# Moving the loads of a scan's B and C rows from SP's queue to ScalarE's

## The chip, the cores and the metric

The kernel runs on one core of a Trainium2 chip. The metric is the device time of one execution in microseconds (us). The engines are called PE (matmul; PEld are its weight loads), DVE or VectorE, ACT or ScalarE, POOL or GpSimd, and SP, which computes nothing and issues transfers (DMAs). ScalarE issues some transfers too, from the same in-order queue that holds its activations.

## What is computed

A stack of eight gated blocks on x (4 batches of 512 tokens by 512 features), with a context of 512 by 256 per batch. Each block adds tanh(gate) times a sub-layer of the normalised x:

```python
x = x + tanh(g_xattn[0]) * L0_xattn(ctx, ln(x))    # a selective scan (Mamba)
x = x + tanh(g_ffn[0])   * L0_ffn(ln(x))           # gated MLP, 2:4 sparsified
x = x + tanh(g_xattn[1]) * L1_xattn(ln(x), ctx)    # attention of the context on itself
x = x + tanh(g_ffn[1])   * L1_ffn(ln(x))           # gated MLP, ternary weights
x = x + tanh(g_xattn[2]) * L2_xattn(ctx, ln(x))    # a selective scan again
x = x + tanh(g_ffn[2])   * L2_ffn(ln(x))           # gated MLP, fp8 weights
x = x + tanh(g_xattn[3]) * L3_xattn(ln(x), ctx)    # 16-head cross attention
x = x + tanh(g_ffn[3])   * L3_ffn(ln(x))           # quantised MLP
```

The part that matters here is the scan of blocks 0 and 4. For each batch, with 512 inner channels and 16 states:

```python
state = state * exp(d_t[..., None] * A) + (d_t * u_t)[..., None] * B_t[:, None, :]
y_t   = einsum('ben,bn->be', state, C_t)
```

d and u are per channel and time; B and C are per state and time, the same for all channels. The scan depends on the context alone, not on x; x enters through the factor silu(ln(x)) that its result is multiplied with.

## The kernel before

There are eight scans: two layers (0 and 1, for blocks 0 and 4) by four batches. A tile is 128 partitions by 512 times, so a scan has 4 channel tiles (d = 0 to 3) by 16 states (n = 0 to 15), 64 steps. One step is `state` and a sum: ScalarE writes exp(d * A) into a PSUM bank (line 570), POOL multiplies du with the row of B (line 571, into `db`), VectorE runs the recurrence along time (line 572, in place in PSUM) and multiplies with the row of C (line 573), and POOL adds the product to y (line 590). The bank comes from a pool of two (`mbps`), which the preparation of later scans (`mamba_pre`) shares.

The rows of B and C for state n are loaded by `bc_tile` (lines 561 to 565): one transfer that reads 2 rows of 512 from DRAM and writes them to all 128 partitions, 512 KB, into a tile with the tag `bc`. There are two such buffers (line 1217). A load for state n therefore waits until VectorE's last product (line 573, d = 3) of state n - 2 has been computed, and POOL's first product of state n waits for the load. The four steps of one state use one `bc` tile.

The first scan (layer 0, batch 0) runs in the prologue in another form, `mamba_scan_pe`, with PE adding up y. The other seven are `mamba_scan`, a generator. They are side work: the main path (attention and MLPs of the batch at hand) calls `tick` after each of its pieces, and `tick` takes steps from the side list at a given rate, 1.2 units a step. Side work gets a priority 1000 places behind the main path (`BEHIND`, from the second phase on). The framework then puts each engine's instructions in an order by a planning run of its own: of what is ready, the instruction with the lowest priority number goes first. What it planned is a fixed order per engine; on the chip each engine, SP and ScalarE's issues included, works its list off in that order and waits where something isn't there.

A scan has to be complete before the head that uses it starts (`Head.start` calls `finish`), which happens in the last matmuls of the MLP or the attention of the batch before. Six heads follow each other while scans run; from about 2390 us on there are none left, and the last heads and the quantised MLPs run alone.

SP issues nearly all transfers in one queue: weights (`unit`, `unit8`, `plain`, lines 259 to 305), stores and loads of the scans' preparation (`copy`, line 247), the scans' d, du and y (line 583), attention's keys and values (line 905), and `bc`. ScalarE issues 188 stores (`keep`, line 252), each right after the activation that wrote its data.

Of the kernel before, what the change touches and what calls it, by code (L numbers as in the profile page):

```python
# [24 lines left out]
NST = 16  # L25
# [50 lines left out]
def tile_flamingo(ctx: ExitStack, tc: tile.TileContext, I, out):  # L76
    nc = tc.nc
    v, s, g, pe, sy = nc.vector, nc.scalar, nc.gpsimd, nc.tensor, nc.sync
# [26 lines left out]
    def nm(base):  # L105
        uid[0] += 1
        return f"{base}_{uid[0]}"

    def T(p, shape, dt, tag, name=None):
        return p.tile(shape, dt, tag=tag, name=nm(name or tag))  # L110
# [95 lines left out]
    for l in range(2):  # L206
# [5 lines left out]
        c = cp.tile([128, 20], F32, name=f"cw{l}")  # L212
# [30 lines left out]
    def copy(dst, src):  # L243

        behind = COPIES if phase[0] else COPIES_FIRST
        tc.cur_priority += behind
        sy.dma_start(dst, src)
        tc.cur_priority -= behind
# [309 lines left out]
            yield 3.4  # L558
        mst[l, b] = bcd, sc

    def bc_tile(bcd, n, p, bufs):

        bc = p.tile([128, 2, 512], F32, tag="bc", name=nm("bc"), bufs=bufs)
        sy.dma_start(bc, bcd.rearrange("(c n) l -> n c l", c=2)[n].partition_broadcast(128))
        return bc

    def state(l, b, n, d, dt, du, bc, db):

        ps = mbps()
        s.activation(ps, dt, AF.Exp, scale=nA[l][:, d * 16 + n : d * 16 + n + 1])  # L570
        g.tensor_tensor(db, du, bc[:, 0], op=MUL)
        v.tensor_tensor_scan(ps, ps, db, 0.0, MUL, ADD)
        v.tensor_tensor(db, ps, bc[:, 1], op=MUL)  # L573

    def mamba_scan(l, b, mp, red):

        M = lambda tag: T(mp, [128, 512], F32, tag)
        bcd, sc = mst[l, b]
        dts, us, ys = [], [], []
        for d in range(4):  # L580
            for tag, r, src in (("dt", dts, sc[d][0]), ("du", us, sc[d][1]), ("y", ys, ysc[l, b][d])):
                x = M(tag)
                copy(x, src)
                r.append(x)
        for n in range(NST):
            bc = bc_tile(bcd, n, mp, mbufs["bc"])
            for d in range(4):
                db = T(mp, [128, 512], F32, "db", f"db{l}{b}x")
                state(l, b, n, d, dts[d], us[d], bc, db)
                red(d).tensor_tensor(ys[d], ys[d], db, op=ADD)  # L590
                yield 1.2
        for d in range(4):
            copy(ysc[l, b][d], ys[d])

    def mamba_scan_pe(l, b, pp):

        bcd, sc = mst[l, b]
        yp = [bank("y", "yp") for d in range(4)]
        for q in range(0, NST, 4):
            bcs = [bc_tile(bcd, n, pp, 6) for n in range(q, q + 4)]  # L600
            for d in range(4):
                if q == 0:
                    pe.matmul(yp[d], ident, sc[d][2], start=True, stop=False)
                for n in range(q, q + 4):
                    db = pp.tile([128, 512], F32, tag="db", name=nm(f"db{l}{b}x"), bufs=5)
                    state(l, b, n, d, sc[d][0], sc[d][1], bcs[n - q], db)
                    pe.matmul(yp[d], ident, db, start=False, stop=n == NST - 1)
                    yield
        ysc[l, b] = yp
# [606 lines left out]
    mp = mctx.enter_context(tc.tile_pool(name="m", bufs=4))  # L1216
    mbufs = {"bc": 2, "mt": 4, "db": 3, "fc": 2, "fw": 2, "kn": 4, "fv": 4, "sq": 1}
# [50 lines left out]
    for h in heads[1:]:  # L1268
        side.append(((h.l, h.b), mamba_scan(h.l, h.b, mp, on_g)))
        pres.append(((h.l, h.b, "pre"), mamba_pre(h.l, h.b, mp)))  # L1270
# [108 lines left out]
```

## Time and profile before

| | |
|---|---|
| time, median of 3 runs (lowest, highest) | 3700.73 us (3695.64, 3701.61) |
| the profiled execution | 3697.43 us, of it 3695.6 us from the first to the last instruction |
| granted TensorE clock, mean | 0.929 |
| busy in 190 to 2400 us (2210 us): PE, DVE, ACT, POOL | 1816.50, 1729.76, 1193.44, 1432.27 us |
| busy in 2400 to 3696 us (1296 us): PE, DVE, ACT, POOL | 1164.84, 639.38, 674.50, 225.29 us |
| exponential of line 570, mean | 690 ns |
| POOL's product with B, median | 1.27 to 1.29 us |
| VectorE's recurrence and product with C, median | 1.22 and 0.68 us |
| issue of a `bc` load on SP, shortest / median / longest | 359 / 371 / 1463 ns |
| a `bc` load, issue to landing, shortest / median / longest | 4.6 / 6.1 / 11.1 us |

How to read what the prediction shows: a row of the waits names the waiting engine, the tile it was about to write and its line, then what ended the wait; the numbers are us in total, how many times, and the longest. `SPq` and `ACTq` are transfers issued on SP's and ScalarE's queue. `db11x` is the product tile of the scan of layer 1, batch 1. A timeline row has the start, the length, the engine, the line, the operation, output <- inputs, and in brackets the engine's idle time before it with what ended it. Rows of stretches have their own legend where they stand.

### The profile page before, as it was taken

The numbers are of one execution on the slowest core, as the hardware profiler recorded it, in microseconds if no ns is written. First come the engines' busy times: TensorE is split into PE (matmuls) and PEld (weight loads), VectorE is DVE, ScalarE is ACT, GpSimd is POOL, SyncE is SP. The second block draws the span as 40 slices with busy tenths as digits, with TensorE's granted clock in tenths as the row PEclk, the third lists the DMA queues.
The fourth block names the chain that finished last, engine by engine and source line by source line (L and its number), as shares of the span: only waits on it lengthen the run. The fifth ranks groups of instructions, "written<-read, shape, count | busy, mean of one in ns | idle before, by whom it ended". The sixth has DMA issues, their size and how long they took to land. (4 is left out here: it accounts for less than half of the span.)

```text
span 3695.6 us, 40240 instructions
## 1 busy us (share of the span) xinstructions
PE 3121.5 (84%) x12216; PEld 1982.6 (54%) x12216; DVE 2535.7 (69%) x4162; ACT 1971.7 (53%) x4371; POOL 1762.6 (48%) x1387
## 2 busy tenths in 40 slices
PE   7787778787886798988878887799998898998995
PEld 3365355563654554574646544475766554664542
DVE  7968766987779868887587888754334446554437
ACT  6455365453632766645544756543435666456644
POOL 4616865757656656646475699600101122212112
PEclk8898899898998999999889999899999999999997
DMA  7667559776755664585656553386654343454311
GB/s 267 235 236 266 175 188 315 252 233 192 239 180 196 214 192 126 177 281 154 229 189 211 179 158 94 111 293 228 227 199 157 109 125 120 150 169 135 114 37 36
DMA packets 303737, 682.62 MB, mean 185 GB/s; under 512 B 31104, under 2 KB 32512, under 8 KB 303520
## 3 DMA queue, kind: packets, MB, share of 16 engines
q1 hardware_dynamic: 278240, 634.43, 52.8%
q10 hardware_dynamic: 25280, 45.63, 3.3%
q8 instruction: 97, 1.59, 0.2%
q14 instruction: 120, 0.98, 0.1%
HBM read 514.97 MB, written 164.95 MB: 184 GB/s over the span
## 5 line engine op out<-in xcount | busy, mean ns | idle before, releaser
L570 ACT ACTIVATE mb<-dt,nA 128x512 f32<-128x512 f32 x512 | 347.9, 690 | 419.6 <-DVE db03x L573 61.5
L323 POOL TENSOR_TENSOR sm<-sm,mhalf 128x8 f32<-128x8 f32 (+4 forms) x96 | 140.6, 1465 | 521.4 <-DVE sm L353 208.5
L663 PE MATMUL gate<-xT,w 128*128 128x512 f32 x624 | 267.0, 428 | 71.1 <-DVE t L730 30.3
L961 PE MATMUL po<-pt,v 128*128 128x512 f32 x512 | 269.6, 628 | 52.7 <-ACT pt L803 49.8
L786 PE MATMUL S<-k,q 128*128 128x512 f32 x512 | 269.2, 627 | 31.7 <-ACT P L793 23.2
L392 PE MATMUL acc<-w,hf 128*128 128x512 f32 x512 | 240.3, 628 | 44.5 <-DVE x L419 14.1
L664 PE MATMUL gate<-xT,w 128*128 128x512 f32 x624 | 257.3, 413 | 1.0 <-DVE xT L257 1.0
L793 ACT ACTIVATE P<-S,st,sm 128x512 f32<-128x512 f32 x256 | 200.3, 785 | 98.4 <-DVE st L791 94.6
L663 PE MATMUL up<-xT,w 128*128 128x512 f32 x624 | 247.5, 397 | 0.6 <-DVE h L731 0.4
L664 PE MATMUL up<-xT,w 128*128 128x512 f32 x624 | 247.1, 396 | 0.0
L787 DVE TENSOR_REDUCE st<-S 128x1 f32<-128x512 f32 x256 | 173.9, 685 | 95.6 <-PE S L786 94.4
L979 PE MATMUL down<-wo,h 128*128 128x512 f32 x512 | 234.4, 609 | 0.8 <-DVE h L970 0.5
L323 POOL TENSOR_TENSOR sml<-sml,mhalf 128x1 f32<-128x1 f32 x32 | 18.5, 579 | 425.1 <-DVE sml L1150 218.4
L392 PEld LDWEIGHTS acc<-w,hf 128*128 128x128 f32 x512 | 102.0, 202 | 177.5 <-issue 120.8
L801 PEld LDWEIGHTS pT<-ident,P 128*128 128x128 f32 x1024 | 127.6, 144 | 128.1 <-issue 64.1
L961 PEld LDWEIGHTS po<-pt,v 128*128 128x128 f32 x512 | 89.4, 194 | 185.1 <-ACT pt L803 146.1
L801 PE MATMUL pT<-ident,P 128*128 128x128 f32 x1024 | 158.4, 280 | 33.3 <-ACT P L793 27.2
L663 PEld LDWEIGHTS gate<-xT,w 128*128 128x128 f32 x624 | 125.0, 200 | 112.4 <-issue 32.4
L803 ACT COPY pt<-pT 128x512 f32<-128x512 f32 x256 | 143.8, 588 | 64.4 <-PE pT L801 63.9
L666 PE MATMUL gate<-xT,w 128*128 128x512 f32 x432 | 174.9, 405 | 3.8 <-POOL w L257 3.8
L666 PE MATMUL up<-xT,w 128*128 128x512 f32 x432 | 169.3, 392 | 0.0
L392 PE MATMUL acc<-w,h 128*128 128x512 f32 x352 | 161.9, 612 | 8.7 <-DVE x L426 5.1
(290 smaller groups left out, 9058.1 us busy)
## 6 DMA issues: line engine op xcount, KB each, us to landing
bc<-dbc SPq DMA_DIRECT2D x128, 512.0 KB, 6.1
w<-dL_g SPq DMA_DIRECT2D x81, 512.0 KB, 5.5
w<-dL_u SPq DMA_DIRECT2D x81, 512.0 KB, 5.1
w<-in_L_d_dram SPq DMA_DIRECT2D x60, 512.0 KB, 5.4
w<-dL_q SPq DMA_DIRECT2D x48, 512.0 KB, 5.3
w<-dL_gu SPq DMA_DIRECT2D x36, 512.0 KB, 4.9
rep<-in_L_b_dram SPq DMA_DIRECT2D x65, 256.0 KB, 3.8
dv<-fv ACTq DMA_DIRECT2D x64, 256.0 KB, 4.7
```

The source lines that it names most:

```text
L323: g.tensor_tensor(a, a, mhalf[:, :n], op=ALU.pow)
L392: pe.matmul(ps, h[:, c], w, start=first, stop=last)
L570: s.activation(ps, dt, AF.Exp, scale=nA[l][:, d * 16 + n : d * 16 + n + 1])
L663: pe.matmul(ps, wh[:, c], xT[k][:, 0], start=k == 0, stop=False)
L664: pe.matmul(ps, wh[:, c], xT[k][:, 1], start=False, stop=wl is None and k == 3)
L666: pe.matmul(ps, wl[:, c], xT[k][:, 0], start=False, stop=k == 3)
L786: pe.matmul(ps, q[:, c], k, start=True, stop=True)
L787: v.tensor_reduce(st[:, t : t + 1], ps, AX.X, ALU.max, negate=True)
L793: s.activation(p, ps, AF.Exp, scale=r, bias=m, accum_out=st[:, 8 + t : 9 + t])
L801: pe.transpose(ps[:, t * 128 : t * 128 + 128], pt[t][:, kt * 128 : kt * 128 + 128], ident)
L961: pe.matmul(po, vs[kt][:, c], u, start=kt == 0, stop=kt == 3)
L979: pe.matmul(ps, hs[j][:, c], ws[j // 2][:, j % 2], start=j == 0, stop=j == 3)
```

## The change

`bc_tile` gets the queue as an argument, SP by default. In `mamba_scan` the tile of the first state is loaded on SP before the loop, as before. Each later one is now loaded from ScalarE's queue and written down earlier: after the sum of d = 1 of the state before it (not for the last state), where it stood at the head of its own state. The number of buffers stays two, and the prologue's scan is untouched.

```diff
-    def bc_tile(bcd, n, p, bufs):
+    def bc_tile(bcd, n, p, bufs, queue=sy):

         bc = p.tile([128, 2, 512], F32, tag="bc", name=nm("bc"), bufs=bufs)
-        sy.dma_start(bc, bcd.rearrange("(c n) l -> n c l", c=2)[n].partition_broadcast(128))
+        queue.dma_start(bc, bcd.rearrange("(c n) l -> n c l", c=2)[n].partition_broadcast(128))
         return bc
...
+        ahead = bc_tile(bcd, 0, mp, mbufs["bc"])
         for n in range(NST):
-            bc = bc_tile(bcd, n, mp, mbufs["bc"])
+            bc = ahead
             for d in range(4):
                 db = T(mp, [128, 512], F32, "db", f"db{l}{b}x")
                 state(l, b, n, d, dts[d], us[d], bc, db)
                 red(d).tensor_tensor(ys[d], ys[d], db, op=ADD)
+                if d == 1 and n + 1 < NST:
+
+                    ahead = bc_tile(bcd, n + 1, mp, mbufs["bc"], s)
                 yield 1.2
```

## The prediction

> **What bounds the kernel now.** I read the page first, then busy time by stretches, the waits of POOL and of SP's queue, the rows of line 564, and last the timelines of three engines around one late load.
>
> ```profile
> span 3695.6 us, 40240 instructions
> PE 3121.5 (84%) x12216; PEld 1982.6 (54%) x12216; DVE 2535.7 (69%) x4162; ACT 1971.7 (53%) x4371; POOL 1762.6 (48%) x1387
> ...
> bc<-dbc SPq DMA_DIRECT2D x128, 512.0 KB, 6.1
> ```
>
> No engine is full over the whole span, so the stage decides. The seven scans that the change touches run from 279 to 2388 us, and their stretches differ (columns: length, then PE, PEld, DVE, ACT, POOL busy, granted clock, DMA share, GB/s):
>
> ```profile
> 1557.00:1576.00 19.00, 19.00 (x81) 14.38 (x80) 10.66 (x19) 7.08 (x14) 2.99 (x3) 1.00 0.89 302
> 1841.00:1852.00 11.00, 11.00 (x50) 9.07 (x49) 1.78 (x2) 2.77 (x10) 3.12 (x3) 1.00 0.97 324
> 660.00:680.00 20.00, 9.31 (x32) 7.50 (x33) 19.77 (x27) 8.46 (x14) 19.31 (x17) 0.66 0.86 291
> 1860.00:1880.00 20.00, 9.01 (x37) 6.87 (x36) 19.75 (x26) 12.71 (x35) 19.45 (x16) 0.83 0.74 237
> 2140.00:2160.00 20.00, 11.81 (x28) 5.72 (x27) 17.31 (x21) 6.67 (x12) 19.65 (x16) 0.74 0.33 105
> ```
>
> The first two are stretches in which PE is full and POOL nearly idle; the other three, two of them near the end of a scan, have POOL at 19.3 to 19.65 of 20 us and PE at about half. So what a scan loses while PE is full is partly paid back in a stretch where POOL sets the pace. POOL loses time to the loads that move, and SP's queue stands in front of them:
>
> ```profile
> POOL db11x L571 <- DMA bc<-dbc: 16.0, 1, 16.0
> POOL db03x L571 <- DMA bc<-dbc: 15.0, 2, 8.8
> POOL db10x L571 <- DMA bc<-dbc: 13.8, 1, 13.8
> POOL db02x L571 <- DMA bc<-dbc: 11.9, 3, 8.0
> ```
>
> ```profile
> SPq L564 <- DVE db13x L573: 111.6, 14, 19.1
> SPq L564 <- DVE db03x L573: 59.6, 10, 12.9
> ...
> SPq L564 <- DMA dv<-fv: 2.8, 1, 2.8
> ```
>
> The second block is SP's own queue: it stands still until VectorE's last product of the scan step before last frees the buffer. Its last line matters below: a bc load waited for the landing of a store issued by ScalarE that has nothing to do with it.
>
> One late load, on ScalarE, SP and POOL:
>
> ```profile
> 1544.15 0.69 ACT L570 ACTIVATE mb<-dt,nA 128x512 f32<-128x512 f32 x1 [1.68 <-DVE db11x L573]
> ```
>
> ```profile
> 1557.61 0.32 SPq L247 DMA_DIRECT2D du<-mt  x1
> 1558.02 1.42 SPq L271 DMA_DIRECT2D w<-dL_u  x1
> ...
> 1567.46 0.38 SPq L564 DMA_DIRECT2D bc<-dbc  x1
> ```
>
> ```profile
> 1573.79 3.78 POOL L571 TENSOR_TENSOR db11x<-du,bc 128x512 f32<-128x512 f32 x3 [16.01 <-DMA bc<-dbc]
> ```
>
> VectorE freed the bc buffer at 1544.1, and that same event released the exponential at 1544.15, the one for d = 1. SP came to the load 23.3 us later, behind weight loads and a store that waited for other engines. POOL paid 16.01 us.
>
> **The change part by part.**
>
> *Which loads move.* 15 of 16 in each of seven scans, 105. The prologue's 16 and each scan's first stay on SP. No instruction is added or removed.
>
> *When they can go.* I paired the 105 loads with the end of the product that frees their buffer and with the exponential of d = 1 before them. In most pairs that exponential starts within 0.2 us of the freeing or later, since its PSUM bank is freed by the same product. So a load put behind it finds its buffer free: this wait on ScalarE's queue costs 0.
>
> *What POOL gets back.* POOL's waits for bc inside these scans, from the timelines: 13.8 (at 706), 8.0, 2.6, 1.4 (1208 to 1297), 16.0 (1574), 6.2 (1647), 8.8 (1849), 5.9 (1958), 4.1 and 1.0 (576, 449): 67.8 us. The freeing lay 10 to 23 us ahead of the issue in the large ones, and a load lands in 6.1 us, so nearly all of it can go. What reaches the end is less. Bounds: 0, because in 1557 to 1576 and 1841 to 1852 PE did not lose anything; 67.8 if POOL's time is the scan's time and the scan ends the stage. I take half for the scans whose later stretches are POOL's (13.8 + 6.2 + 8.8 + 5.9 + 4.1 = 38.8), since PE runs at about half there, and nothing for the rest: -19 us. What POOL waits for next is VectorE's product for the sum of line 590, which already holds it 65 us in one scan (db03x), so a scan can't gain more than the loads cost it.
>
> *What lies behind the loads on SP.* SP stood 395.5 us at line 564 between 190 and 2400. The weight, store and scan loads behind it can go earlier. Those few waits that engines have for such transfers bound it: ScalarE for mt<-ddtp 48.6 us (20.3 of them where a new head starts, which stays), POOL for dst<-mt 28.0. Weight loads have seven buffers, and PE's waits for them sum to tens of us over the whole kernel. I take 0, with 0 to -10 for the range.
>
> *Issue time on ScalarE.* Stores that ScalarE issues took 326 ns (median), the bc load on SP 371 ns: 105 x 0.37 = 39 us of its queue. The load needs no result of the exponential ahead of it; stores in this trace start about 0.1 us after the start of an unrelated activation ahead of them. 0.1 + 0.37 is less than that activation's 0.69, so I take 0. If the cover is gone, up to 39 us of an engine that is 54% busy in this stage: at the same half, 20 us.
>
> *A new wait on ScalarE.* All transfers of both queues signal eight semaphores in turn (241 each here), and none of the 1920 that have one eight places before starts before that one has landed. So ScalarE's load waits for the transfer eight places earlier, often one on SP's queue, and behind it stand evictions and exponentials for PE, VectorE and POOL. From the nearest row, the 188 stores that ScalarE issues today: five waited over 0.5 us, 2.7 at most, about 8 us in all, so 105 x 8 / 188 = 4 to 5 us, half of it felt: +2. From the other side, if each load keeps its place in the common order but ScalarE reaches it at its exponential: 16 of 105 wait, 135 us in all, the longest 19.3 and 18.6. I take +2, by the stores, because they are on that very queue and interleaved with the same loads, and keep +67 (half of 135) for the range.
>
> *A rule that speaks against.* The Trainium skill, "DMA: Bandwidth & Descriptors", section "Issuing engines are not separate DMA queues", says that issuing from several engines saves only the sequencer's issue time, which is usually small. By that the change is worth 0 and the time 3701. The rows of SP show another thing than bandwidth, an in-order queue that held one load for 23.3 us, which the rule leaves out.
>
> *Sum.* -19 + 0 + 0 + 2 = -17. The profiled execution took 3697.4 us, 3.3 below the median of the three runs. 3697.4 - 17 + 3.3 = 3684.
>
> **The rivals.** *Nothing measurable* (13%). The waits for bc fall where PE is full, as in 1557 to 1576, and a scan that ends sooner only waits for its head's turn. Against it: the stretches with POOL at 97%. About 3701.
>
> *ScalarE stalls at the shared semaphores* (32%). Place: a bc load in ScalarE's queue whose eighth predecessor is a weight load that SP can't issue yet, because PE has not freed its buffer; PE in turn needs the evictions behind the stall. For it: SP came late (over 4 us) to nineteen bc loads. Against it: five real waits among 188 stores. Price: up to 67, minus the gain of 19: 3701 + 67 - 19 = 3749 at the full price, 3732 where three quarters are paid. It decides from about 40 us of stalls on ScalarE, since half of that cancels the 19.
>
> *The order shifts* (13%). The order of instructions on each engine is planned, with side work 1000 places of priority behind; another queue for 105 transfers gives another order from 330 us on. Either sign, about 20 us: 3680 or 3720, split 6 and 7.
>
> The forecast holds 42%. Chances: faster 0.42 + 0.06 = 0.48; within 0.2% (7.4 us, about what a measurement of this kernel can tell from no change) 0.13; slower 0.32 + 0.07 = 0.39. The likeliest case has its own range, 3662 to 3693: with 40 us of POOL's time felt at the low end and with 10 of stalls at the other. The range for 8 in 10, 3658 to 3745, leaves out about 7% below (more of the 67.8 felt, SP's relief of 10 on top) and 12% above (the semaphores at nearly full price, the issue uncovered).
>
> **What would show it.** Right: POOL's waits for bc fall from 67.8 to under 15 us; bc rows stand on ScalarE's queue within 1 us of an exponential of line 570; the stretches with POOL full and PE half get shorter; line 564 leaves SP's waits but for the first of each scan. Wrong: waits of ScalarE for transfers (today 2.8 us for a store is the longest on its queue) grow to tens of us; PE's waits for evictions of gate, kn or pt grow by as much; SP's waits move unchanged to the next load. The likeliest error is the half: if PE takes back none of POOL's time, the answer is no change.

## The result, and the profile after

The changed kernel takes 3714.92 us (median of 16 runs, 3710.95 to 3726.86) against 3705.33 us for the kernel before (16 runs, 3695.64 to 3714.15): ratio 1.0027, 95% interval 1.0018 to 1.0037. It is slower, by 7 to 14 us. The forecast was 3684.

The page of the kernel after, its span, busy times and the moved loads:

```profile
span 3712.0 us, 40225 instructions
...
PE 3123.4 (84%) x12216; PEld 1989.4 (54%) x12216; DVE 2534.2 (68%) x4162; ACT 1967.5 (53%) x4371; POOL 1760.3 (47%) x1387
...
bc<-dbc ACTq DMA_DIRECT2D x105, 512.0 KB, 5.7
```

All busy times are within 7 us of before, those of PE, VectorE, ScalarE and POOL within 5. What grew is idle time. The loads did what they should: the waits of POOL for them, and SP's waits at their line, in the kernel after (us in total, times, longest; the first row of the second block is from before):

```profile
POOL db11x L571 <- DMA bc<-dbc: 4.8, 3, 2.7
POOL db03x L571 <- DMA bc<-dbc: 3.7, 4, 1.5
POOL db10x L571 <- DMA bc<-dbc: 2.9, 3, 1.8
...
POOL db02x L571 <- DMA bc<-dbc: 0.5, 2, 0.3
```

```profile
SPq L905 <- PE S L786: 168.9, 38, 14.0
...
SPq L909 <- PE S L790: 260.3, 42, 20.0
...
SPq L564 <- DVE db00x L573: 15.0, 10, 4.0
SPq L564 <- DMA dbc<-mt: 5.0, 1, 5.0
SPq L564 <- DVE db11x L573: 0.9, 1, 0.9
```

POOL's waits for `bc` in the seven scans fell from 70.5 to 15.8 us (the 70.5 are the prediction's 67.8 and 2.7 for the first load of one scan, which does not move). SP stands 1 us at line 564 there, where it stood 395.5; the rows of `db00x` and `dbc` belong to the prologue. But SP only stands elsewhere: its waits for PE at the loads of attention's keys and values (line 909, 905 before) rose from 168.9 to 260.3 us, and all its waits from 190 to 2410 us come to some 1780 us, against 1700 before.

Where the time went, by stages that end with a scan; first before, then after (columns: length, then PE, PEld, DVE, ACT, POOL busy, granted clock, DMA share, GB/s):

```profile
893.00:1308.00 415.00, 326.97 (x1303) 226.94 (x1302) 339.77 (x509) 206.42 (x465) 261.90 (x199) 0.91 0.65 217
1308.00:1604.00 296.00, 266.37 (x1063) 162.63 (x1062) 232.69 (x367) 179.78 (x400) 186.65 (x149) 0.95 0.55 170
...
1927.00:2185.00 258.00, 217.01 (x921) 146.01 (x919) 210.58 (x312) 149.17 (x317) 180.92 (x144) 0.93 0.57 184
...
2389.00:3696.00 1307.00, 1175.23 (x5053) 739.36 (x5051) 642.30 (x1412) 677.95 (x1556) 227.37 (x190) 0.96 0.46 151
```

```profile
900.00:1335.00 435.00, 337.42 (x1314) 233.08 (x1314) 339.94 (x512) 206.57 (x466) 262.71 (x201) 0.89 0.63 210
1335.00:1622.00 287.00, 255.00 (x1041) 158.79 (x1042) 233.22 (x365) 179.50 (x405) 187.58 (x149) 0.96 0.54 171
...
1943.00:2213.00 270.00, 223.43 (x946) 150.59 (x944) 209.96 (x321) 154.46 (x338) 182.61 (x145) 0.91 0.55 179
...
2415.00:3712.00 1297.00, 1164.37 (x5018) 734.40 (x5016) 638.70 (x1408) 679.07 (x1558) 226.08 (x190) 0.96 0.46 150
```

These are one execution of each kernel. The stage of the scan `db02x` loses 20 us, that of `db12x` 12, and 7 are lost ahead of these; the stage of `db11x` wins 9 and the rest behind the last scan 10. A cost at the loads themselves would be spread over seven scans, with 15 loads in each. This one sits for the most part in two stages, and a comparison of the two traces row by row shows why that is possible: the planning run made another order. At the least, 840 of VectorE's 4162 rows would have to change their place to give the order of before, 368 of PE's 12216 and 600 of ScalarE's 4371, the loads not counted.

On ScalarE's queue one of the two longest waits ahead of a moved load, timeline of the kernel after:

```profile
1623.04 0.69 ACT L570 ACTIVATE mb<-dt,nA 128x512 f32<-128x512 f32 x1
1625.40 0.39 ACTq L564 DMA_DIRECT2D bc<-dbc  x1
1625.96 0.64 ACT L718 ACTIVATE ha<-hf 128x512 f32<-128x512 f32 x1 [2.22 <-DVE hf L716]
```

The load went 1.7 us after the activation ahead of it had ended, and 2.3 us after ScalarE could have issued it, if that is taken as 0.1 us after the start of the activation ahead (where its stores start in before). Counted like that, only eight of the 105 came over 0.5 us late, and all waits ahead of the 105 sum to some 14 us.

### The profile page after: what moved, and what is told of

Its sections match the earlier page's. It is cut to its first block, busy times and chain, and to the rows that moved or that the text cites. A ratio compares the mean times of both kernels' runs of the same rounds, so it can differ in the third digit from the quotient of the medians.

```text
span 3712.0 us, 40225 instructions
## 1 busy us (share of the span) xinstructions
PE 3123.4 (84%) x12216; PEld 1989.4 (54%) x12216; DVE 2534.2 (68%) x4162; ACT 1967.5 (53%) x4371; POOL 1760.3 (47%) x1387
## 5 line engine op out<-in xcount | busy, mean ns | idle before, releaser
L667 PE MATMUL gate<-xT,w 128*128 128x512 f32 x624 | 267.9, 429 | 81.2 <-DVE t L734 33.9
L668 PE MATMUL gate<-xT,w 128*128 128x512 f32 x624 | 260.8, 418 | 1.9 <-DVE xT L257 1.8
L670 PE MATMUL gate<-xT,w 128*128 128x512 f32 x432 | 178.6, 413 | 10.2 <-POOL w L257 10.2
```

The costliest lines, as they stand in the source:

```text
L667: pe.matmul(ps, wh[:, c], xT[k][:, 0], start=k == 0, stop=False)
L668: pe.matmul(ps, wh[:, c], xT[k][:, 1], start=False, stop=wl is None and k == 3)
L670: pe.matmul(ps, wl[:, c], xT[k][:, 0], start=False, stop=k == 3)
```

## The experiments

### How the order was held

Most kernels below hold the order of all other work fixed. The program is planned twice: once in the form whose order is wanted, then as the kernel to be run, with edges of order (no waits) between neighbours on each engine. Only the loads are free to be placed. The core of it (condensed, as are the other cuts of code below):

```python
plan = planned(arrays, PLAN)               # each engine's order, without the loads
for a, b in zip(order, order[1:]):         # in the second pass, engine by engine
    tc.add_manual_dep(mine[e][b], mine[e][a].name, why, reason="plan")
```

So "order of before" means that PE, VectorE, ScalarE, POOL and SP issue everything but these loads in exactly the sequence of the kernel before; the traces of e1, e5, e6, e10 and e13 show it row by row, without one exchange. In these kernels the lines stand some 5 to 26 further down than in before; the tile names are the same. "Small" is a load of 64 columns of B (32 KB in place of 512); the row of C is left out, and both products read these 64 columns eight times over. `d = 1` names the step of the state before behind which a load is written; without it the load stands at the head of its own state.

| kernel | loads on | order | median us (runs) | ratio to before, 95% interval |
|---|---|---|---|---|
| after | ScalarE, d = 1 | its own | 3714.9 (16) | 1.0027 (1.0018, 1.0037) |
| e1 | ScalarE, d = 1 | before's | 3724.9 (5) | 1.0054 (1.0041, 1.0067) |
| e2 | SP | after's | 3771.2 (4) | 1.0177 (1.0162, 1.0191) |
| e3 | SP, d = 1 | its own | 3690.6 (6) | 0.9963 (0.9950, 0.9977) |
| e4 | ScalarE, own state | its own | 3704.3 (11) | 0.9999 (0.9987, 1.0010) |
| e5 | SP, and 32 bytes on ScalarE | before's | 3708.0 (12) | 1.0005 (0.9993, 1.0017) |
| e6 | ScalarE, and 32 bytes on SP | before's | 3732.9 (6) | 1.0076 (1.0058, 1.0094) |
| e7 | SP, and plain activations | before's | 3707.3 (12) | 1.0008 (0.9997, 1.0020) |
| e8 | SP, d = 1 | before's | 3707.9 (12) | 1.0007 (0.9996, 1.0018) |
| e9 | SP, small | before's | 3683.3 (6) | 0.9932 (0.9919, 0.9946) |
| e10 | ScalarE, small | before's | 3689.9 (5) | 0.9957 (0.9945, 0.9969) |
| e11 | none | before's | 3679.9 (6) | 0.9933 (0.9919, 0.9947) |
| e12 | ScalarE, d = 3 | its own | 3701.1 (10) | 0.9986 (0.9976, 0.9995) |
| e13 | ScalarE, small, e1's places | before's | 3677.0 (5) | 0.9917 (0.9899, 0.9935) |
| e14 | ScalarE, small, after's places | after's | 3697.4 (10) | 0.9964 (0.9953, 0.9976) |
| e15 | ScalarE, d = 0 | its own | 3686.8 (4) | 0.9940 (0.9921, 0.9959) |
| e16 | SP, d = 0 | its own | 3693.6 (6) | 0.9959 (0.9941, 0.9977) |
| e17 | ScalarE, d = 0 | before's | 3716.0 (6) | 1.0037 (1.0023, 1.0050) |
| e18 | ScalarE, d = 2 | its own | 3698.1 (10) | 0.9993 (0.9981, 1.0005) |

The kernel before ran beside each group (medians 3703.4 to 3707.8); differences in us below are of medians, against the before of the same group, and can stand some 3 us from what the ratio gives. An interval is 4 to 7 us to either side, so a difference between two of these kernels is known to about 8 us, and what is made of two such differences to some 10.

### Queue and order taken apart (e1 to e4)

The theory after the first comparison of the traces: the new order costs what the change lost, and the queue itself gains.

e1, before's order with the loads on ScalarE:

```diff
+PLAN = ('sy', -1)    # order of: loads on SP, each at the head of its state
+MAKE = ('s', 1)      # build: loads on ScalarE, behind d == 1
```

> The 105 loads on ScalarE's queue, every other instruction of the five engines in the order of the kernel before. Theory O (the order, planned anew for the moved loads, costs what the change lost; the queue itself gains): 3685 to 3700 us, faster than before by 0.15 to 0.5%, POOL's waits for bc in the scans under 20 us. Rival Q (the issue time of 40 us and the waits ahead of the loads on ScalarE cost it): about 3715, like the kernel after. Rival N (what POOL gets back never reaches the end, and the queue costs nothing): within 0.1% of before, 3702 to 3709.

e2, the reverse:

```diff
+PLAN = ('s', 1)
+MAKE = ('sy', -1)
```

> The order of the kernel after on all five engines, with the 105 loads back on SP's queue, each issued for its own state as before. Theory O: as slow as the kernel after or slower, 3713 to 3735, since the order's cost stays and the gain goes. Rival Q: as before, 3700 to 3708, since ScalarE is free of the loads. Rival N: 3713 to 3717, as after.

e3, the place in the program alone:

```diff
-                    ahead = bc_tile(bcd, n + 1, mp, mbufs["bc"], s)
+                    ahead = bc_tile(bcd, n + 1, mp, mbufs["bc"], sy)
```

> The place of the loads alone: each is written behind d = 1 of the state before, as in the kernel after, but stays on SP's queue; the planner makes its own order, which stands close to that of before (19 of 11670 of PE's instructions out of order, 85 of 4164 of VectorE's). All theories: within 0.2% of before, 3698 to 3712. POOL's waits for bc stay above 40 us if SP's queue, and not the place in the program, makes the loads late.

e4, the queue without the early place (against before):

```diff
-            bc = bc_tile(bcd, n, mp, mbufs["bc"])
+            bc = bc_tile(bcd, n, mp, mbufs["bc"], s if n else sy)
```

> The queue without the early place: the 105 loads on ScalarE's queue, each written at the head of its own state; the planner makes its own order (794 of PE's 11670 instructions out of order against before, 371 against after). Theory O: another order, so another time, anywhere in 3690 to 3725, not tied to 3715. Rival Q: 3713 to 3725, at least as slow as after, because each load is issued by the same queue and waits longer there. Rival N: 3702 to 3709.

The theory fell at once: e1 came out above what any of the three had expected. In before's order the loads on ScalarE's queue cost 18.5 us (e1), so the new order of the kernel after does not cost anything against e1, it saves some 9. But after's order with the loads on SP is 65 us slower than before (e2): each of the two orders did worse with the other's queue. And e3, which leaves the loads on SP and shifts only their place in the program, is 16 us faster, which nobody expected. Rival Q seemed to be left: something about ScalarE's queue.

e1 also shows what became of POOL's gain. POOL in e1, at the load that prediction and before's trace show with a wait of 16.01 us:

```profile
1575.42 3.77 POOL L578 TENSOR_TENSOR db11x<-du,bc 128x512 f32<-128x512 f32 x3
1603.70 1.66 POOL L599 TENSOR_TENSOR y<-y,db11x 128x512 f32<-128x512 f32 x1 [24.52 <-DVE db11x L580]
```

and the sum behind the same load in before:

```profile
1582.32 1.66 POOL L590 TENSOR_TENSOR y<-y,db11x 128x512 f32<-128x512 f32 x1 [4.76 <-DVE db11x L573]
```

The products start without a wait, and POOL then waits 24.52 us for VectorE's product, where it waited 4.76 in before. Over the scans POOL's waits for `bc` fell to 15 us, its waits for VectorE's products at the sum rose from 242 to 300.

### Is it ScalarE's time, or SP's relief? (e5 to e8)

e5: ScalarE issues 105 transfers at the moved loads' places, with the same wait for the buffer and a turn at the shared semaphores, but the real loads stay on SP.

```diff
+        flat = p.tile([128, 1032], F32, tag="bc", name=nm("bc"), bufs=bufs)
+        bc = flat[:, :1024].rearrange("p (c l) -> p c l", c=2)
+        s.dma_start(flat[0:1, 1024:1032], bcd[n : n + 1, 0:8])     # behind d == 1
         sy.dma_start(bc, ...)                                      # its old place
```

> Order of before on every engine; the 105 real loads stay on SP's queue at their old place, and ScalarE issues 105 loads of 32 bytes (one packet) into a spare strip of the same buffers, at the places that the moved loads had, with the same wait for the buffer and for the shared semaphores. Theory I (issuing 105 transfers, and waiting for them to be allowed, takes ScalarE's time from evictions and exponentials): 3718 to 3730, as slow as the loads on ScalarE in before's order (3725). Theory R (SP, rid of the loads, issues weights and stores sooner, and these collide with others): 3702 to 3710, like before.

e6: the same with the two queues exchanged, so that SP stands for the buffer as before.

```diff
+        s.dma_start(bc, ...)                                       # behind d == 1
+        sy.dma_start(flat[0:1, 1024:1032], bcd[n : n + 1, 0:8])    # the old place
```

> Order of before; the 105 real loads on ScalarE's queue, and SP issues a load of 32 bytes into a spare strip of the same buffer at the old place of each, so that SP's queue stands for the buffer as it did before. Theory I: 3720 to 3735, the cost on ScalarE is untouched. Theory R: 3690 to 3708, since SP's other transfers go at their old times.

e7: the time alone.

```diff
                 state(l, b, n, d, dts[d], us[d], bc, db)
+                if d == 1 and n + 1 < NST:
+                    s.activation(idle, ident, AF.Copy, scale=ones[:, 0:1])
```

> Order of before, loads on SP as before, and 105 activations of 128x128 (0.3 to 0.39 us each by the rows of lines 870 and 878, 32 to 41 us in all) that nobody waits for on ScalarE, at the places of the moved loads: the issue time alone, without any transfer or semaphore. Theory I in the form that the time itself counts: 3716 to 3728 (about half of the 32 to 41 us). In the form that the waits ahead of the loads count (16 us on ScalarE): 3704 to 3712. Theory R: 3702 to 3712.

e8: e3's place, in before's order.

```diff
+PLAN = ('sy', -1)
+MAKE = ('sy', 1)
```

> Order of before on every engine for all but the loads, which stay on SP's queue but are written behind d = 1 of the state before; SP issues some of them earlier. If the 16 us that this place gained came from the loads: 3687 to 3695. If they came from the few other instructions that the planner moved: 3702 to 3709.

The group of e7's added activations (count, then busy us and mean ns), and the tiny transfers in e5's list of issues:

```profile
L604 ACT ACTIVATE idle<-ident,ones 128x128 bf16<-128x128 f32 x105 | 41.1, 391 | 0.0
```

```profile
bc<-dbc SPq DMA_DIRECT2D x128, 512.0 KB
...
bc<-dbc ACTq DMA_DIRECT2D x105, 0.0 KB
```

41.1 us more work on ScalarE cost 1.9 us (e7, interval -1 to 7). 105 more issues, 24.9 us of issue time and some 17 us of waits ahead of them, cost 2.7 (e5, -3 to 6). So theory I is out in both its forms. Theory R is out too: with SP held as before, the loads on ScalarE cost 27.5 us (e6), not less than in e1. The 9 us more than e1 are one load that stood late on ScalarE's queue in this kernel: POOL waited 20.56 us for it at 965 us, and e6 falls some 10 us behind e1 within that stretch. e8 says that e3's gain was not the loads' place either but the few instructions that the planning run moved (in its trace 166 of VectorE's 4162 rows and 30 of PE's 12216).

What is left is the transfer itself. e1 and before issue the same instructions in the same order, so each transfer can be compared with itself. I paired each issue on SP with the update of its semaphore that says it has landed, for the 914 transfers other than `bc` between 280 and 2400 us (us from issue to landing, before taken as the mean of before and e7):

| runs beside a `bc` load | transfers | in before | in e1 |
|---|---|---|---|
| in neither | 393 | 4.07 | 4.08 |
| only in e1 | 138 | 4.75 | 6.19 |
| only in before | 91 | 5.25 | 4.42 |
| in both | 292 | 5.66 | 5.49 |

Sorted by whether a `bc` load is under way when the transfer is issued, which a late landing can't change, the rows say the same (130 transfers that have one in e1 alone: 6.73 us, 4.47 in before). Over all 914 the mean rises only from 4.80 to 4.88 us, since others come sooner: what changes is which transfers are late.

A load in its own queue no longer stands behind the transfers that SP issues, it runs beside them and takes their place. How that reaches PE; timeline of before, where the `bc` load followed the weights `fw`:

```profile
1011.53 1.01 SPq L271 DMA_DIRECT2D fw<-dL_v  x2
...
1015.45 0.42 SPq L564 DMA_DIRECT2D bc<-dbc  x1
...
1017.53 0.47 PE L326 MATMUL V<-fw,fc 128*128 128x512 f32 x1
```

and of e1, where it went ahead of them:

```profile
1015.10 0.42 ACTq L569 DMA_DIRECT2D bc<-dbc  x1
...
1016.02 0.90 SPq L276 DMA_DIRECT2D fw<-dL_v  x2
...
1025.65 0.77 PE L331 MATMUL V<-fw,fc 128*128 128x512 f32 x1 [3.71 <-DMA fw<-dL_v]
```

The two `fw` landed 5.86 and 6.43 us after their issue in before, 9.49 and 10.30 in e1. PE, which had not waited, waits 3.71 us. One pair of rows does not part the `bc` load from SP's own transfers, which also stand closer together there in e1; e13, below, does. The same happens 240 us earlier to a store of a scan's preparation (`dst`, 4.16 us to landing in before, 6.15 in e1): POOL waits 2 us longer for it, VectorE for POOL, ScalarE for VectorE, and PE for ScalarE's eviction `fv` (8.55 us in place of 6.59).

### The bytes (e9 to e11, e13, e14)

If that is the cost, it must go with the bytes. "Small" loads carry a sixteenth.

```diff
-        i = queue.dma_start(bc, bcd.rearrange("(c n) l -> n c l", c=2)[n].partition_broadcast(128))
+        i = queue.dma_start(bc[:, 0, :64], bcd[n : n + 1, :64].rearrange("o l -> (o l)").partition_broadcast(128))
...
+        b = bc[:, 0, :64].unsqueeze(1).to_broadcast([128, 8, 64])
-    g.tensor_tensor(db, du, bc[:, 0], op=MUL)
+    g.tensor_tensor(cut(db), cut(du), b, op=MUL)
```

> Order of before. Each of the 105 loads carries 64 columns of B alone (32 KB in place of 512 KB), and the two products read these 64 columns eight times over; C and the other columns are left out. Loads on SP's queue at their old place. This is the base for the next: 3690 to 3708, since POOL still waits for SP's queue but 50 MB less are moved.

> The same small loads (64 columns of B, the rest left out) on ScalarE's queue, order of before. Theory C (the full loads, once they go sooner and on their own, run beside other transfers that someone waits for, and make these land later: that is the cost of the 19 us between before and before's order with ScalarE's queue): with a sixteenth of the bytes the cost is gone, 12 us faster to 3 us slower than the same loads on SP. Theory P (products of POOL that come sooner cost the others something, whatever the bytes): 14 to 25 us slower than the same loads on SP.

e11 has no loads behind the first state:

```diff
-            bc = bc_tile(bcd, n, mp, mbufs["bc"])
+            bc = ahead          # the rows of state 0
```

> Order of before; the 105 loads are left out, and every state of a scan uses the rows of state 0. No product of POOL waits for a load any more, and nothing of theirs is in the way: the most that better loads could give. If half of POOL's 38.8 us reaches the end, as the prediction took it: 3660 to 3690. If next to nothing does (POOL then waits for VectorE's products instead): 3695 to 3706.

e10 fell between its two theories, 6.6 us slower than e9. One of its loads stood late on ScalarE's queue, and POOL waited 17 us for it. e13 puts the small loads at exactly the places of e1's full ones, e14 does the same with the kernel after (a second planning pass holds the loads too):

```diff
+    plan = planned(arrays, ("sy", -1, ""))                # order of before
+    plan = planned(arrays, ("s", 1, ""), plan, True)      # with e1's places of the loads
+    return planned(arrays, ("s", 1, "small"), plan)
```

> Order of before, the small loads (64 columns of B, the rest left out) on ScalarE's queue at exactly the places that the full loads had there (3724.9 us); in the small loads on ScalarE before this, one stood elsewhere and POOL waited 17 us for it. If the bytes beside other transfers are the whole of the 19 us: 3676 to 3686, as the small loads on SP (3683.3) or faster. If the place of one load was not the rest, and the queue costs some us without bytes: 3688 to 3694 as before.

> The kernel after with every instruction in its very order, the 105 loads on ScalarE's queue cut to 64 columns of B (the rest left out). If the bytes of these loads beside other transfers are what holds the kernel after at 3715: 3675 to 3690, a fall of 25 to 40 us, more than the 23 that the same cut gave in before. If the new order is what holds it: 3690 to 3710, a fall of under 23.

In before's order the bytes cost 23 us on SP's queue (before to e9) and 49 on ScalarE's (e1 to e13, 18.5 + 30.8). Without them ScalarE's queue is no worse than SP's (e13 30.8 us under before, e9 23.0; the difference is not known from zero). That settles e1: all of its loss goes with the bytes of the loads. It is not the other way of reading B and C: POOL's and VectorE's products take 1276 and 678 ns in e13, 1276 and 679 in before (medians). And e13 shows the places looked at above with the same order and the same places of the loads: the two `fw` land after 6.10 and 6.71 us (9.49 and 10.30 in e1) and PE waits 0.27 us for them in place of 3.71, `dst` lands after 4.58 (6.15), and the 138 transfers take 5.06 us (6.19).

The same runs price POOL's waits. POOL's waits for `bc` in e9:

```profile
POOL db11x L584 <- DMA bc<-dbc: 15.4, 1, 15.4
POOL db10x L584 <- DMA bc<-dbc: 10.2, 1, 10.2
POOL db03x L584 <- DMA bc<-dbc: 8.7, 2, 7.0
```

and what POOL waits for in e11, where there is no load to wait for:

```profile
POOL y L599 <- DVE db03x L580: 71.3, 17, 17.6
POOL y L599 <- DVE db12x L580: 52.0, 13, 18.9
POOL y L599 <- DVE db11x L580: 47.7, 21, 19.4
POOL y L599 <- DVE db10x L580: 41.6, 11, 12.8
```

e9 still waits 46.6 us for loads and e11 not at all, and the two are equal (0.9932 and 0.9933). The waits have gone to VectorE's products (those of `db11x` 36.8 us in before, `db10x` 28.7). Taken by itself e11 would not show this: its 3679.9 us lie in the range that its expectation gave to the prediction's half. Only e9, which keeps two thirds of the waits and moves a sixteenth of the bytes, has nearly all of that gain too. What is open is the rest of the way: from before to e9 POOL's waits fell as well, from 70.5 to 46.6 us, and no run parts these 24 us from the bytes.

e14 missed my larger guess: small loads take 20 us off the kernel after (in medians against before, 9.6 and -10.4), no more than the 23 in before. So in its own order the bytes cost the kernel after no more than they cost before; what holds it is the order. e13 and e14 differ in nothing but order, the places of the loads included, and by 20 us. Where, in one stage of each, first e13, then e14:

```profile
893.00:1301.00 408.00, 324.99 (x1287) 224.72 (x1287) 336.26 (x505) 204.43 (x459) 258.19 (x196) 0.90 0.59 201
```

```profile
893.00:1324.00 431.00, 333.63 (x1314) 230.01 (x1314) 338.53 (x510) 206.65 (x466) 260.83 (x198) 0.89 0.58 194
```

It is the stage of `db02x` again, where the kernel after had lost its 20 us. PE's waits there for one kind of eviction, e13 and e14:

```profile
PE K L331 <- ACT fv L916: 8.6, 4, 3.2
```

```profile
PE K L331 <- ACT fv L916: 13.0, 3, 8.5
```

The kernel after has 14.8 us there with the same longest wait of 8.5, before 10.0 and 3.6. This is one of several small waits; which instruction's place begins it was not tried.

### How much an order is worth (e12, e15 to e18)

e12, e15 and e18 are the kernel after with `d == 3`, `d == 0` and `d == 2`; e16 is e3 with `d == 0`; e17 is e1 with `d == 0`:

```diff
-                if d == 1 and n + 1 < NST:
+                if d == 0 and n + 1 < NST:
```

> As the kernel after, but the loads on ScalarE's queue are written behind d = 3 of the state before in place of d = 1; the planner makes its own order. With loads on ScalarE's queue three orders gave 3725 (before's order), 3715 (after) and 3704 (each load at the head of its own state). If the order is chance within such a band: 3700 to 3725.

> As the kernel after, the loads behind d = 0 of the state before, the planner's own order. Loads on ScalarE's queue gave 3725, 3715, 3704 and 3701 in four orders. An order by chance: 3698 to 3726.

> Loads on SP's queue, written behind d = 0 of the state before, the planner's own order (45 of PE's 11670 instructions and 162 of VectorE's 4164 out of order against before). Loads on SP gave 3706 and 3691 in two orders. If orders with the loads on SP are no better than those with ScalarE's but for chance: 3690 to 3720; if SP's queue is better by the 19 us that the fixed order shows: 3685 to 3708.

> Order of before, loads on ScalarE's queue behind d = 0. Behind d = 1 in this order: 3725. The loads behind d = 0 in the planner's own order gave 3687, with 112 us of waits ahead of them on ScalarE. If that gain came from the place (sooner loads): under 3705. If it came from the order: 3720 to 3740, with the cost of the fixed order and perhaps of ScalarE's waits on top.

> As the kernel after, the loads behind d = 2, the planner's own order. The other places on ScalarE's queue gave 3687 (d = 0), 3715 (d = 1), 3701 (d = 3) and 3704 (head of the own state), which follows no order of the places. By chance of the order: 3685 to 3718.

With loads on ScalarE's queue and an order of its own for each place, the times against before are -21 (d = 0), +10 (d = 1, the change), -5 (d = 2), -5 (d = 3) and -2 us (own state). They follow no order of the places; by its interval, that of d = 2 and of the own state are no difference. In before's order the places d = 0 and d = 1 give +13 and +18.5, not known to differ; the 34 us between e17 and e15, both with d = 0, come with the order. e15 is the fastest complete kernel here, 0.9940 (0.9921 to 0.9959), below what its expectation had allowed, though its loads stand long on ScalarE, some 112 us in all ahead of the 105 issues. The same holds for e17, and e1, in the same order, has 18: the 94 us more of these waits did not make e17 slower than e1. The longest, in e15's timeline:

```profile
1654.63 0.68 ACT L570 ACTIVATE mb<-dt,nA 128x512 f32<-128x512 f32 x1
1662.06 0.38 ACTq L564 DMA_DIRECT2D bc<-dbc  x1
1663.21 0.63 ACT L718 ACTIVATE ha<-hf 128x512 f32<-128x512 f32 x1 [7.90 <-DVE hf L716]
```

The load went 6.7 us after the activation ahead had ended, and the activation behind it waited 7.9 us for VectorE, so this wait cost nothing.

## Why the prediction was wrong

*Which loads move, and when they can go.* Right. 105 are on ScalarE's queue, and 97 of them go within half a microsecond of the earliest time that ScalarE could issue them, as counted above.

*What POOL gets back.* The waits fell nearly as told, from 67.8 us to 15.8 at most. The step that failed is the next one, "half for the scans whose later stretches are POOL's": -19. With the loads' bytes nearly out of the way, POOL waits 46.6 us less in e11 than in e9, and the time is the same; it waits 44 us less in e13 than in e9, and the 8 us between them are not known from zero. For the full loads no run shows it apart from their bytes. The text had named what takes the waits' place, VectorE's product at the sum, and called the half the likeliest error. What misled it was to read stretches with POOL at 97% as a rate that sets the end: POOL's order there holds sums that need VectorE, and the waits went there (e1's 24.52 us, e11's rows).

*SP's relief, 0 to -10.* Not told apart from zero. SP's waits moved on to other lines, to the scans' copies (line 247), the weights and line 909 (168.9 to 260.3 us); that was one of the signs of being wrong that the prediction named. Theory R, that the relief costs something, fell with e6.

*Issue time, 0.* Right: 41.1 us of added activations cost 1.9.

*The wait at the shared semaphores, +2, and its rival with 32%.* The term was not contradicted, the rival's price was wrong: 2.7 us, known to 5, for all 105 issues with their waits (e5). The kernel after has some 14 us of stalls; e17 has 94 us more of them than e1 in the same order and is no slower. (That none of 1920 transfers starts before the one eight places ahead has landed holds in the trace but for three, by up to 1.1 us.)

*The missing term.* No step of the sum asked what the moved loads run beside once they no longer stand in SP's queue. In before's order that is worth +26 (49 less 23), known to some 10, and it alone turns e1 to the wrong side. The rule that the prediction weighed, the Trainium skill, "DMA: Bandwidth & Descriptors", "Issuing engines are not separate DMA queues", has two halves. I argued with the second, that only issue time is saved. The first says that transfers of all issuing engines run on the same 16 DMA engines and interleave; that a moved load gets in the way of others, the rows of e1 show: 6.19 us against 4.75 for the 138 transfers that got a `bc` load beside them.

*The order, 13%, either sign, some 20 us.* This rival came nearest: 3720 was its slow end, 3714.9 the time. That the number came so near is in part luck, since bytes and queue are in it too. It cannot be added up in one way only. From before, in before's order: the queue with its bytes +18.5, then the new order -9. Or: bytes out -23, queue -8, order +20, bytes in +20. Both end near +10; queue, bytes and order act together, as e2's 65 us show most plainly. What the runs show is that the order planned for d = 1 is the slowest of five planned for this queue, and that with each of the other four the loads on ScalarE's queue measured faster than before or no different.

## What to carry to other kernels

A wait that an engine loses is worth only what the next wait in its fixed order leaves of it: take the loads out altogether first, and that one run bounds the gain. A load that leaves a shared queue also loses its place behind the transfers that others wait for; list what it will run beside. Where a planner orders the program, hold the order and change one thing, then let it plan anew for several equal forms of the change, since here five such orders lay 31 us apart, three times the loss to be explained.

## What the runs showed of the hardware

Transfers of two queues slow each other, and the mean DMA share of a stage does not tell where. It was 0.65 in the stage of `db02x` before, yet around the late `fw` of e1 the DMA engines were full (columns as above: length, PE, PEld, DVE, ACT, POOL busy, granted clock, DMA share, GB/s):

```profile
1015.00:1021.00 6.00, 6.00 (x28) 4.93 (x27) 5.96 (x9) 3.21 (x7) 5.52 (x5) 1.00 0.91 259
1021.00:1025.60 4.60, 0.94 (x5) 0.44 (x3) 2.85 (x5) 2.83 (x11) 2.86 (x3) 0.84 1.01 390
1025.60:1031.00 5.40, 5.35 (x13) 4.12 (x14) 1.94 (x2) 3.19 (x11) 5.40 (x4) 0.51 0.65 245
```

There a 512 KB load of `fw` took 9.49 us, in place of 5.86 in before and of 6.10 in e13, where the `bc` load ahead of it is small. A high share alone is no sign of a late load either: it was 0.90 in before from 1011 to 1017 us. ScalarE, 53% busy, took 105 added activations or 105 added issues with no loss that could be measured.

PE is slower where it stands more: in the stage of `db02x` it was busy 326.97 us for 1303 recorded matmuls at a granted clock of 0.91 before, and 337.42 us for 1314 at 0.89 after, by estimate about 8 us of the 20 lost there. The rows above have one such place. Behind PE's wait of 3.71 us the granted clock is 0.51 for 5.4 us, and the matmuls go 0.43 us apart where they went 0.23 ahead of it. In e17, where PE waits 2.68 us at the same place, it stays 1.00 (1021.4 to 1026.5 us), and in e13, with 0.27 us, too (1014.4 to 1020). Whether the clock follows the idle time everywhere or has another cause was not tried.
